# A macaron block on one core: the start, up to the second superblock, rewritten with a held order and a split of the ternary weights into absolute value and sign

## The chip, the cores and the metric

The kernel runs on one core of one Trainium2 chip. The metric is the device time of one execution in microseconds, as a median of runs. The engines are named as in the profile: PE is TensorE (matrix products), PEld its weight loads, DVE is VectorE, ACT is ScalarE, POOL is GpSimd, and SP issues most of the DMAs. Each engine takes its own queue of instructions strictly in order; an instruction that waits holds up all that stand behind it.

## The reference

The input is x of 16 sequences x 256 tokens x 256 features. Three layers follow each other, each with a residual:

```python
x = x + 0.5 * ffn(layernorm(x))
x = x + attention(layernorm(x))      # 16 heads of 16, 4 key groups, causal
x = x + 0.5 * ffn(layernorm(x))      # the same weights again

def ternary_quant(w):
    scale = jnp.mean(jnp.abs(w)) + 1e-8
    return jnp.clip(jnp.round(w / scale), -1.0, 1.0) * scale

def ffn(x):                          # W_up, W_gate: 1024 x 256, W_down: 256 x 1024
    up, gate = x @ ternary_quant(W_up).T, x @ ternary_quant(W_gate).T
    return (silu(up) * gate) @ ternary_quant(W_down).T
```

Before the first product of a weight matrix can run, its mean absolute value must therefore be known over all of its 262,144 elements, and each element must be turned into -1, 0 or 1, by comparing it with plus and minus half the scale.

## The kernel before

The 4096 tokens are cut into eight superblocks of 512. One feed-forward pass over a superblock has eight *units*, f = 0 to 7, each for 128 of the 1024 hidden features, and four *downs*, one for each 128 tokens.

- A unit (`ffn_unit`, line 464) computes `up` and `gate`, four products of 128x512 each (line 451; the normalized input is held as a high and a low f16 half, for two chunks of features). ACT takes the activation of `up` into `th` (line 480), DVE multiplies it with `gate` into `h` (line 481), ACT writes the high f16 half of `h` into `hT` (line 491), and POOL writes the low half (line 492).
- A down (`ffn_down`, line 496) is 16 products of 128x256 with the ternary `td` (line 502), and DVE adds the result to x (line 507). A superblock's four downs are 64 products.

**Order.** A planner (`run`, line 891) writes the steps out in an order, from costs and due times written by hand, with a main chain of units and downs (`ffn_chain`, line 769) and side chains for the norms, the projections and the attention. Behind it a scheduler orders the instructions of each engine again, by its own estimate of their times, unless they are pinned (`pin`, line 223) or of high priority. The result is fixed in the program. Steps for the start are inserted into the main chain at places given by numbers (lines 1047 to 1053).

**The start.** SP issues the loads: x of superblock 0 in one piece, W_up in four, W_gate in one, x of superblock 1, W_down, then the rest (lines 190 to 205). POOL fills constant tiles for the attention. TensorE runs 12 small products to be busy (line 219). The norm of a superblock is: statistics on DVE (line 332), a power of -0.5 on POOL (line 339), the normalization on ACT and DVE (lines 347 and 352), and then, for superblocks 0 and 1, transposes on TensorE and a split into high (ACT) and low (DVE) halves (lines 386 to 389); from superblock 2 on the halves are written into `xparts` (ACT line 364, POOL line 367) and transposed by a DMA.

**The ternary weights before.** `ternary_sums` (line 277) adds up absolute values, on ACT mostly, with a throw-away output. `ternary_scale` (line 298) sums over the partitions by a product with ones (line 301) and makes the two bounds `hi` and `lo`. `ternary_piece` (line 312) makes one quarter of a matrix in two steps:

```python
if engine == "a":
    nc.scalar.activation(dn, wi, AF.Relu, bias=lo, scale=-1.0)
    nc.scalar.activation(dn, dn, AF.Sign)
else:
    by.tensor_scalar(dn, wi, lo, None, ALU.is_lt)      # by: gpsimd or vector
nc.vector.scalar_tensor_tensor(ti, wi, hi, dn, ALU.is_gt, ALU.subtract)
```

So `dn` (is w below -scale/2?) needs the scale. For W_up all four quarters of `dn` are made on DVE; for W_gate one on DVE, two on ACT, one on POOL; for W_down all four on ACT. The second step is always on DVE.

For the projections' weights, DVE finds maxima (`projections_most`, line 980), TensorE transposes them (`mt`, line 998) and later spreads them with a product (`every`, line 1007).

Of the kernel before, what the change touches and what calls it, by code (L numbers as in the profile page):

```python
# [25 lines left out]
ENG_U = "vvvv"  # L26
ENG_G = "vapa"
ENG_D = "aaaa"
NUF = "000000"
NWF = "404000"  # L30
# [8 lines left out]
PINF = 0  # L39
NW4 = 0  # L40
PRE = 0
USUM = 1
GSUM = 0
PING = 0
HPU = 0
GFIRST = 0
PINF1 = 0
TDA = 1
PINK = 1
KM = 2  # L50
KV = 12
PINA = 0
PINM = 1
PINT = 0
NWARM = 12
NWARM2 = 0
NWARM3 = 0
GCUT = 0
# [9 lines left out]
C1 = 1  # L68
C2 = 4
C3 = 5  # L70
TD = 6
DR = 6
DS = 2
PM = 9
# [3 lines left out]
GU = 1  # L78
# [15 lines left out]
NORM = 1024.0  # L94


@with_exitstack
def macaron_kernel(
# [45 lines left out]

    x_t = x.rearrange("(n s) (t p) e -> n p (s t) e", s=2, t=2)
# [44 lines left out]
    load_x(0)  # L190
    for w, w_t in ((wu, w_upT), (wg, w_gateT)):
        for i in range(NCUT if w is wu or GCUT else 1):
            nn = NCUT if w is wu or GCUT else 1
            cut = slice(i * F // nn, (i + 1) * F // nn)
            nc.sync.dma_start(w[:, :, cut], w_t.rearrange("(c p) f -> p c f", p=P)[:, :, cut])
# [13 lines left out]
    nc.vector.tensor_copy(identh, ident)  # L209
    ones = const.tile([P, P], F32, tag="ones", name="ones")  # L210
    nc.vector.memset(ones, 1.0)
    neg_half = const.tile([P, TT], F32, tag="neg_half", name="neg_half")
    nc.vector.memset(neg_half, -0.5)

    def warm(n, name):
        if n:
            pw = bank([P, P], f"warm_{name}")
            for _ in range(n):
                nc.tensor.matmul(pw, ones, ones, start=True, stop=True)

    warm(NWARM, "start")
# [4 lines left out]

    box = {}
# [10 lines left out]
    def constant_rows():  # L238
# [4 lines left out]
        nc.gpsimd.memset(k[KP:KR], 0.0)  # L243
        ku = k[KP:KR].rearrange("p (v u k) -> p v u k", v=3, k=U)
        for which, base in ((EVEN, 0), (ODD, 32)):
            nc.gpsimd.affine_select(
                out=ku[:, which], in_=ku[:, which], pattern=[[0, S // U], [-1, U]],
                compare_op=ALU.is_ge, fill=-MASK, base=base, channel_multiplier=1,
            )
        nc.gpsimd.memset(k[KR : KR + 3], -MROW)  # L250
        nc.gpsimd.memset(v[KP:KR], 0.0)
        vj = v[KP:KR].rearrange("p (j b) -> p j b", b=4)
        nc.gpsimd.affine_select(
            out=vj, in_=vj, pattern=[[1, 32], [0, 4]], compare_op=ALU.not_equal,
            fill=MASK, base=0, channel_multiplier=-1,
        )
        for to in Ks:
            nc.sync.dma_start(
                to[KP : KR + 3].rearrange("p g v k -> p g (v k)"),
                k[KP : KR + 3].unsqueeze(1).to_broadcast([KR + 3 - KP, G, 3 * S]),  # L260
            )
        box["queries"] = v

    def constant_values():
        for v in VT:
            nc.gpsimd.memset(v, 0.0)
            nc.gpsimd.memset(v[:, :, :, D : D + 1], 1.0)
# [9 lines left out]
    def ternary_sums(w, name):  # L277
        if name == "d":
            cuts = [(w[:, : FC // 2], 1), (w[:, FC // 2 :], 1)]
        elif name == "u" or GCUT:  # L280
            fq = F // NCUT
            cuts = [(w[:, :, i * fq : (i + 1) * fq], 0 if i % 2 == 0 and not USUM else 1) for i in range(NCUT - 1)]
            h = fq // 2
            cuts += [(w[:, :, (NCUT - 1) * fq : (NCUT - 1) * fq + h], 0), (w[:, :, (NCUT - 1) * fq + h :], 1)]
        else:
            cuts = [(w[:, : EC // 2], GSUM), (w[:, EC // 2 :], 1)]
        part = small.tile([P, len(cuts)], F32, tag="part", name=f"part_{name}")
        for i, (piece, on_scalar) in enumerate(cuts):
            if on_scalar:
                junk = fp.tile([P] + list(piece.shape[1:]), F16, tag="th", name=f"junk_{name}_{i}")  # L290
                nc.scalar.activation(junk, piece, AF.Abs, accum_out=part[:, i : i + 1])
            else:
                pin(PING and name == "g", nc.vector.tensor_reduce(
                    part[:, i : i + 1], piece, AX.XY, ALU.add, apply_absolute_value=True
                ))
        return part

    def ternary_scale(w, name, part):
        n = w.shape[1] * w.shape[2]
        allsum = bank([P, part.shape[1]], f"allsum_{name}")  # L300
        nc.tensor.matmul(allsum, ones, part, start=True, stop=True)
        tot = small.tile([P, 1], F32, tag="tot", name=f"tot_{name}")
        nc.vector.tensor_reduce(tot, allsum, AX.X, ALU.add)
        s = const.tile([P, 1], F32, tag=f"s_{name}", name=f"s_{name}")
        nc.vector.tensor_scalar(s, tot, 1.0 / (P * n), TERNARY_EPS, ALU.mult, ALU.add)
        hi = small.tile([P, 1], F32, tag="hi", name=f"hi_{name}")
        nc.vector.tensor_scalar(hi, s, 0.5, None, ALU.mult)
        lo = small.tile([P, 1], F32, tag="lo", name=f"lo_{name}")
        nc.vector.tensor_scalar(lo, s, -0.5, None, ALU.mult)
        return s, hi, lo  # L310

    def ternary_piece(wi, ti, hi, lo, name):
        engine = {"u": ENG_U, "g": ENG_G, "d": ENG_D}[name[0]][int(name[1])]
        dn = fp.tile([P] + list(wi.shape[1:]), BF16, tag="tmp", name=f"dn_{name}")
        if engine == "a":
            nc.scalar.activation(dn, wi, AF.Relu, bias=lo, scale=-1.0)
            nc.scalar.activation(dn, dn, AF.Sign)
        else:
            by = nc.gpsimd if engine == "p" else nc.vector
            pin(PINT and engine == "v", by.tensor_scalar(dn, wi, lo, None, ALU.is_lt))  # L320
        nc.vector.scalar_tensor_tensor(ti, wi, hi, dn, ALU.is_gt, ALU.subtract)


    def norm_stages(n, name, factor, finish, early=False):
# [4 lines left out]
        def stats():  # L329
            st = small.tile([P, TT, nc.vector.BN_STATS_DIM], F32, tag="st", name=f"st_{name}")  # L330
            for t in range(TT):
                pin(PINA if name[0] == "a" else PINF1 if name in ("f0_1", "f0_2") else PINF if name[:2] == "f0" else 0, nc.vector.bn_stats(st[:, t, :], xs[n][:, t, :]))
            for t in range(TT):
                nc.vector.bn_aggr(mv[:, t, :], st[:, t, :])
            ve = small.tile([P, TT], F32, tag="ve", name=f"ve_{name}")
            nc.vector.tensor_scalar(
                ve, mv[:, :, 1], LN_EPS, 1.0 / (factor * factor), ALU.add, ALU.mult
            )
            nc.gpsimd.tensor_tensor(rstd, ve, neg_half, ALU.pow)

        def normalize():
            on_scalar = 2 if name in ("first", "second") else NACT0 if early else NACT
            shift = small.tile([P, TT], F32, tag="shift", name=f"shift_{name}")
            nc.vector.scalar_tensor_tensor(shift, mv[:, :, 0], -1.0, rstd, ALU.mult, ALU.mult)
            for t in range(TT):
                if t < on_scalar:
                    nc.scalar.activation(
# [3 lines left out]
                else:  # L351
                    nc.vector.tensor_scalar(  # L352
# [6 lines left out]
    def ffn_norm(n, name, tag="xT", early=False):  # L359
# [3 lines left out]
        def high(xn):  # L363
            nc.scalar.copy(parts[:, 0].rearrange("p c t e -> p t c e"), xn.rearrange("p t (c e) -> p t c e", c=EC))  # L364

        def low(xn):
            nc.gpsimd.tensor_tensor(  # L367
# [9 lines left out]
    def early_norm(n, name):  # L377

        xT = lnp.tile([P, 2 * EC * TT, P], F16, tag="xT", name=f"xT_{name}")
        view = xT.rearrange("p (a c t) q -> p a c (t q)", a=2, c=EC)  # L380

        def transposed(xn):
            for c in range(EC):
                pt = bank([P, TT, P], f"xt_{name}_{c}")
                for t in range(TT):
                    nc.tensor.transpose(pt[:, t, :], xn[:, t, c * P : (c + 1) * P], ident)
                p2 = pt.rearrange("p t q -> p (t q)")
                nc.scalar.copy(view[:, 0, c, :], p2)
                nc.vector.tensor_tensor(view[:, 1, c, :], p2, view[:, 0, c, :], ALU.subtract)

        return view, norm_stages(n, name, NORM, [transposed])
# [43 lines left out]
    def ffn_prepare(key):  # L435
        n, p = key
        if key == order[1]:
            view, stages = early_norm(n, "second")
        else:
            view, stages = ffn_norm(n, f"f{p}_{n}", early=p == 0 and n < EARLY_F)  # L440
# [5 lines left out]
    half_done = {}  # L446

    def products(key, f, w, acc):
        for c in range(EC):
            for a in range(2):  # L450
                nc.tensor.matmul(  # L451
# [4 lines left out]
    def ffn_up(key, f):  # L456
        name = f"{key[1]}_{key[0]}_{f}"
        if key == order[0] and f < 6:
            warm(int(NUF[f]), f"u{f}")
        up = bank([P, 512], f"u_{name}")  # L460
        products(key, f, tu, up)
        half_done[key, f] = up

    def ffn_unit(key, f):
        n, p = key
        name = f"{p}_{n}_{f}"
        if f == 0:
            hidden[key] = hp.tile([P, FC, 2, 512], F16, tag="hT", name=f"hT_{p}_{n}")
        hT = hidden[key]
        if (key, f) not in half_done:  # L470
            ffn_up(key, f)
        up = half_done.pop((key, f))
        gate = bank([P, 512], f"g_{name}")
        if key == order[0] and f < 6:
            warm(int(NWF[f]), f"g{f}")
        products(key, f, tg, gate)
        th = fp.tile([P, 512], F32, tag="th", name=f"th_{name}")
        h = fp.tile([P, 512], F32, tag="h", name=f"h_{name}")
        if key in order[:SILU]:
            nc.scalar.activation(th, up, AF.Silu, scale=scales["one_u"])  # L480
            nc.vector.scalar_tensor_tensor(h, gate, scales["per_u"], th, ALU.mult, ALU.mult)
# [620 lines left out]
```

## Time and profile before

| what | value |
|---|---|
| median of 3 runs | 566.72 us (565.25 to 567.57) |
| the profiled execution's own time | 563.64 us |
| its span in the profile | 561.9 us |
| mean granted TensorE clock | 0.988 |
| PE busy | 539.4 us, 96% of the span |
| DVE, ACT, POOL busy | 433.2, 376.5, 355.0 us (77%, 67%, 63%) |
| first product of superblock 0 (`u`, unit 0) | begins at 13.28 us |
| first products of superblock 1 | begin at 33.23 us |
| first down product of superblock 0 | begins at 47.43 us |
| last down product of superblock 0 ends, unit 5 of superblock 1 begins | 54.59 us in the chain |

How to read it: a row of the profile page's groups gives line, engine, operation, `out<-in` by the program's tile names, the shapes, the count, then the busy time, the mean of one in ns, and the idle time of the engine before it with what ended it. A row of the timeline has the start in us, the duration, the engine, the line, the operation and how many were merged. A row of a table by windows has, for each stretch, the busy time of each engine, the granted TensorE clock (1.00 is full), the busy share of the DMA engines and their GB/s. In the names of tiles, `Qs` is also where the raw W_up, W_gate and W_down lie during the start.

### The profile page before, as it was taken

How to read it: one execution, taken by the hardware profiler on the slowest of the kernel's cores; microseconds unless marked ns; L12 is line 12 of the kernel's file. 1: busy time of each engine (PE TensorE's matmuls, PEld its weight loads, DVE VectorE, ACT ScalarE, POOL GpSimd, SP SyncE). 2: the span in 40 equal slices, each digit the busy share in tenths (PEclk: the TensorE clock that was granted, in tenths of full speed). 3: DMA queues.
4: the chain of work that ended last, by engine and by line, in shares of the span. 5: the costliest groups of instructions: out<-in, count | busy, mean ns of one | idle time of the engine just before them, and what ended most of it. 6: DMA issues, size and time to landing. Idle time of an engine off the chain costs nothing.

```text
span 561.9 us, 12132 instructions
## 1 busy us (share of the span) xinstructions
PE 539.4 (96%) x4593; PEld 331.1 (59%) x4593; DVE 433.2 (77%) x1027; ACT 376.5 (67%) x658; POOL 355.0 (63%) x380
## 2 busy tenths in 40 slices
PE   6979999989999999999999999899999999999997
PEld 5436556647555665655665664566645666565565
DVE  6988878977989899878877798459965697846663
ACT  5894747487689668677856749765599445875642
POOL 4466869556489658766845539854489534865542
PEclk8899999999999999999999999999999999999999
DMA  8933268571059059047339003572023840020201
GB/s 297 297 43 56 38 156 154 125 167 44 3 160 144 1 147 159 3 126 142 47 96 190 12 3 38 135 170 38 3 40 66 205 87 22 12 65 14 67 28 48
DMA packets 119316, 51.25 MB, mean 91 GB/s; under 512 B 85173, under 2 KB 119001, under 8 KB 119257
## 3 DMA queue, kind: packets, MB, share of 16 engines
q1 hardware_dynamic: 118825, 50.08, 40.4%
q8 instruction: 36, 0.59, 0.4%
q10 hardware_dynamic: 432, 0.39, 0.3%
q14 instruction: 23, 0.19, 0.1%
HBM read 22.41 MB, written 14.68 MB: 66 GB/s over the span
## 4 chain that ended last, share of the span: by engine, by line
PE 72%; ACT 10%; DVE 9%; DMA 5%; POOL 2%; issue 2%; SPq 0%; DVEq 0%; ACTq 0%; POOLq 0%
PE d L502 18%; PE u L451 15%; PE g L451 14%; PE o L706 6%; PE s L611 6%; PE st L675 5%; PE qkv L525 4%; ACT pT L676 2%; DMA Qs<-prows 2%; PE ot L722 2%; DVE xn_f L352 1%; DVE h L486 1%; DVE tmp L485 1%; ACT hT L491 1%; DVE tops L625 1%
## 5 line engine op out<-in xcount | busy, mean ns | idle before, releaser
L492 POOL TENSOR_TENSOR hT<-h,hT 128x512 f16<-128x512 f32 x128 | 149.2, 1171 | 88.8 <-ACT hT L491 88.0
L676 ACT ACTIVATE pT<-st,exp_scale 128x512 f32<-128x512 f32 x192 | 119.8, 698 | 26.1 <-PE st L675 26.0
L502 PE MATMUL d<-td,hT 128*128 128x256 f16 x1024 | 122.4, 273 | 0.2 <-ACT pT L676 0.2
L625 DVE TENSOR_REDUCE tops<-s 128x8 f32<-128x512 f32 x160 | 103.1, 678 | 16.1 <-PE s L611 15.7
L451 PE MATMUL u<-xT_f,tu 128*128 128x512 f16 x448 | 115.2, 379 | 0.3 <-DVE h L486 0.3
L451 PE MATMUL g<-xT_f,tg 128*128 128x512 f16 x448 | 115.3, 379 | 0.0
L684 POOL TENSOR_SCALAR_AFFINE_SELECT pT<-pT 128x512 f32<-128x512 f32 x128 | 80.5, 637 | 54.7 <-ACT pT L676 51.7
L491 ACT CAST hT<-h 128x512 f16<-128x512 f32 x128 | 79.5, 621 | 49.2 <-DVE h L486 39.0
L502 PEld LDWEIGHTS <-hT 128*128 128x128 f16 x1024 | 98.4, 98 | 18.0 <-issue 0.5
L485 DVE SCALAR_TENSOR_TENSOR tmp<-th,u 128x512 f32<-128x512 f32 x96 | 65.5, 684 | 50.3 <-ACT th L483 49.8
L483 ACT ACTIVATE th<-u,half_u 128x512 f32<-128x512 f32 x96 | 66.2, 692 | 42.8 <-PE u L451 42.4
L451 PEld LDWEIGHTS <-tg 128*128 128x128 f16 x512 | 50.2, 98 | 61.8 <-issue 1.7
L451 PEld LDWEIGHTS <-tu 128*128 128x128 f16 x512 | 47.6, 99 | 43.7 <-issue 2.9
L486 DVE SCALAR_TENSOR_TENSOR h<-g,tmp 128x512 f32<-128x512 f32 x96 | 65.7, 685 | 5.7 <-PE v L573 0.5
L675 PE MATMUL st<-Qs,ks 99*128 99x512 f16 x192 | 54.1, 380 | 5.4 <-DMA Qs<-prows 2.8
L611 PEld LDWEIGHTS <-Qs 96*128 96x128 f16 x896 | 50.9, 116 | 12.7 <-issue 3.0
L611 PE MATMUL s<-ks,Qs 96*128 96x64 f16 (+2 forms) x896 | 53.3, 208 | 0.0
L706 PE MATMUL o<-pT,vt 128*32 128x128 f32 (+1 forms) x1024 | 49.4, 329 | 0.0
L706 PEld LDWEIGHTS o<-pT,vt 128*32 128x32 f32 x1024 | 28.5, 109 | 25.1 <-issue 8.6
L507 DVE SCALAR_TENSOR_TENSOR x<-d,so,x 128x256 f32<-128x256 f32 x64 | 30.4, 478 | 16.5 <-PE d L502 16.0
L525 PE MATMUL qkv<-xT_a,wparts 128*128 128x512 f16 x144 | 34.7, 379 | 2.0 <-DMA xT_a<-xparts_a 1.9
L367 POOL TENSOR_TENSOR xparts_f<-xn_f,xparts_f 128x1024 f16<-128x1024 f32 x14 | 29.9, 2132 | 9.4 <-ACT xparts_f L364 9.2
(163 smaller groups left out, 605.1 us busy)
## 6 DMA issues: line engine op xcount, KB each, us to landing
qd<-sp SPq DMA_DIRECT2D x32, 256.0 KB, 2.6
Qs<-qd SPq DMA_DIRECT2D x64, 128.0 KB, 3.5
ks<-kd SPq DMA_DIRECT2D x48, 128.0 KB, 4.1
x<-in_x SPq DMA_DIRECT2D x8, 512.0 KB, 8.7
out<-x SPq DMA_DIRECT2D x32, 128.0 KB, 3.0
kd<-sp SPq DMA_DIRECT2D x16, 128.0 KB, 2.5
Qs<-in_w_upT SPq DMA_DIRECT2D x4, 256.0 KB, 4.9
Qs<-in_w_gateT SPq DMA_DIRECT2D x1, 1024.0 KB
```

What stands on the lines that cost most here:

```text
L451: nc.tensor.matmul(acc, w[:, c, f * P : (f + 1) * P], ffn_ready[key][:, a, c, :], start=(c == 0 and a == 0), stop=(c == EC - 1 and a == 1),)
L485: nc.vector.scalar_tensor_tensor(tmp, th, 1.0, up, ALU.add, ALU.mult)
L486: nc.vector.scalar_tensor_tensor(h, gate, 0.25 / (NORM * NORM), tmp, ALU.mult, ALU.mult)
L491: nc.scalar.copy(hT[:, f, 0, :], h)
L492: nc.gpsimd.tensor_tensor(hT[:, f, 1, :], h, hT[:, f, 0, :], ALU.subtract)
L502: nc.tensor.matmul(acc, hT[:, f, a, t * P : (t + 1) * P], td[:, f, :], start=(f == 0 and a == 0), stop=(f == FC - 1 and a == 1),)
L611: nc.tensor.matmul(sc[:, at : at + n, :], Qs[0:KR, b // 4, g * P : (g + 1) * P, b % 4], k[:, g, which, first * U : (first + n) * U], start ...
L625: nc.vector.tensor_reduce(peaks[q][:, u, :], sc, AX.X, ALU.max)
L675: nc.tensor.matmul(sc, keys, mov, start=True, stop=True)
L676: nc.scalar.activation(pT[:, u, :].rearrange("p (h b j) -> p h b j", h=4, b=4), sc.rearrange("p (h j b) -> p h b j", h=4, b=4), AF.Exp, sc ...
L684: nc.gpsimd.affine_select(out=v, in_=v, pattern=[[0, 4], [1, P]], compare_op=ALU.is_ge, fill=0.0, base=0, channel_multiplier=-1,)
L706: pin(not first, nc.tensor.matmul(at[:, half * P :], v[:, 2 * s + half, g, :], moving, start=half == 0, stop=half == 1, tile_position=(0, ...
```

## The change

The start is written anew up to and with the norm statistics of superblock 2, and all that is issued in this stretch keeps the written order on every engine: a wrapper around the engines pins each instruction while a flag is set. What comes behind it is ordered by planner and scheduler as before.

- **Loads.** x of superblock 0 comes in two halves, W_gate in four pieces instead of one; the statistics of superblock 0 run by halves, with two powers on POOL instead of one.
- **Ternary weights.** w becomes `(|w| > scale/2) * (half of the sign of w)`. The half signs (+0.5 or -0.5) need no scale. They are made by POOL from the raw weights, one `tensor_scalar` of two operations for each quarter (128x512), but for the first eighth of W_up, which DVE makes. The absolute values are kept: ACT's sums write them into a tile (`sizes`, in the space of a later `hT`); for W_down they overwrite the raw weights. DVE then needs one instruction for a quarter, with two inputs in SBUF, as before. The `dn` instructions on ACT and DVE are gone. A factor of two that the half signs bring is moved into the scales.
- **Sums.** Some are on DVE (two quarters of W_gate, an eighth of W_up). The sum over partitions accumulates piece by piece in one PSUM bank. The scale and bounds are each made by one DVE instruction from that bank.
- **Activation table.** A one-element Silu is the first activation, so that its table is loaded at the start; the two table loads of the first stretch (at 0.78 and at 16.93 us before, 1.28 us each) become one.
- **Products.** The `up` products of units 0 and 1 are interleaved, chunk by chunk. From there the order is written out: `up` products run one or two units ahead of `gate`, with the sign, size and ternary pieces between them. Seventeen warming products instead of 12 at the start and three before the first `gate`; the eight between units are gone.
- **Constants.** All constant tiles of the attention are filled on POOL before the first norm.
- **W_down.** Its signs, sums and ternary pieces are inserted as steps of the planner after superblock 0 (places 0, 1, and 2 to 5 of the main chain); the projections' maxima and the products behind them come later.

In the built program, POOL's queue after the norm of superblock 0 is: sign of W_up (eighth 2), of W_gate (quarter 1), W_up (2), W_gate (2); then low half of unit 0, sign W_up (3), low 1, sign W_gate (3), low 2, sign W_up (4), the power for superblock 1, low 3, sign W_gate (4), lows 4 to 7; the power for superblock 2, the low half of unit 0 of superblock 1, four signs of W_down, `xparts` of superblock 2, and the lows of units 1 to 7. On ACT the normalization and `xparts` of superblock 2 stand just ahead of the first sum of W_down, which stands ahead of the activation of unit 1 of superblock 1. On PE the product that adds the first half of W_down's sum (`all_d`) stands between units 0 and 1 of superblock 1, the second inside the last products of unit 4; the 64 down products of superblock 0 follow; `mt` and `every` come after them. From the downs of superblock 1 on, PE's order is that of the kernel before.

The core of the diff:

```diff
+    class Engine:
+        def __getattr__(self, name):
...
+            def issue(*args, **kwargs):
+                ins = fn(*args, **kwargs)
+                if box["in_order"]:
+                    tc.keep_in_program_order(ins)
+                return ins
...
-    load_x(0)
+    for s in range(2):
+        nc.sync.dma_start(xs[0][:, 2 * s : 2 * s + 2], x_t[0][:, 2 * s : 2 * s + 2])
...
+    def half_sign(engine, to, w):
+        engine.tensor_scalar(to, w, 0.0, 0.5, ALU.is_ge, ALU.subtract)
+
+    def ternary(t, size, cut, sign):
+        vector.scalar_tensor_tensor(t, size, cut, sign, ALU.is_gt, ALU.mult)
+
+    def affine(name, acc, factor, eps):
+        to = const.tile([P, 1], F32, tag=name, name=name)
+        vector.tensor_scalar(to, acc, factor / (E * F), eps, ALU.mult, ALU.add)
+        return to
...
+    def sum_by_scalar(size, w, part, i, lo, hi):
+        scalar.activation(cut_w(size, lo, hi), cut_w(w, lo, hi), AF.Abs, accum_out=part[:, i : i + 1])
...
+    g_ternary(0, 1)
+    g_ternary(1, 2)
+    s_g = affine("s_g", all_g, 1.0, TERNARY_EPS)
+    warm(NWARM2, "second")
+    units[0].gate()
+    units[1].gate()
+    u_ternary(2, 4)
...
+    units[0].join()
+    size_by_scalar(size_g, wg, 4, 6)
+    split(0)
+    u_sign(gpsimd, 4, 6)
+    next_up(2)
+    g_ternary(2, 4)
+    next_up(3)
...
+    split(3)
+    g_sign(gpsimd, 6, 8)
+    units[4].gate()
+    u_ternary(6, 8)
...
+    g_ternary(6, 8)
+    units[5].join()
...
+    third = ffn_prepare(order[2])
+    third[0]()
+    vector.tensor_copy(identh, ident)
+    box["in_order"] = False
+    for stage in third[1:]:
+        stage()
...
     def ternary_down_sums():
+        for i in range(4):
+            rows = slice(2 * i, 2 * i + 2)
+            half_sign(gpsimd, sign[:, rows], wd[:, rows])
+        for i in range(2):
+            rows = slice(4 * i, 4 * i + 4)
+            scalar.activation(wd[:, rows], wd[:, rows], AF.Abs, accum_out=part[:, i : i + 1])
+
+    def ternary_down_scale():
+        all_d = bank([P, 1], "all_d")
+        for i in range(2):
+            total(all_d, box["part_d"][:, i : i + 1], i == 0, i == 1)
```

## The prediction

> **What bounds the kernel now.** I read the page's head, then the start by windows, then the chain and the waits of the first 56 us.
>
> ```profile
> PE 539.4 (96%) x4593; PEld 331.1 (59%) x4593; DVE 433.2 (77%) x1027; ACT 376.5 (67%) x658; POOL 355.0 (63%) x380
> ...
> PE   6979999989999999999999999899999999999997
> ```
>
> From the fourth slice on PE is full nearly everywhere. Only the start and the end have room, and a microsecond by which PE's queue comes later at 54 us is a microsecond of the end.
>
> ```profile
> 5.00:10.00 5.00, 1.57 (x10) 1.29 (x9) 3.03 (x15) 3.19 (x10) 2.17 (x4) 0.90 1.04 381
> 10.00:15.00 5.00, 4.18 (x18) 3.52 (x19) 5.00 (x16) 2.76 (x6) 0.00 (x0) 0.50 1.09 352
> 15.00:20.00 5.00, 4.33 (x14) 1.62 (x14) 5.00 (x22) 3.78 (x6) 2.07 (x2) 0.57 1.10 347
> ...
> 35.00:40.00 5.00, 1.84 (x9) 0.64 (x7) 4.06 (x7) 5.00 (x9) 2.58 (x2) 0.97 0.00 0
> 40.00:45.00 5.00, 4.61 (x16) 1.93 (x17) 4.19 (x9) 3.84 (x8) 5.00 (x5) 0.68 0.59 108
> ```
>
> Columns: PE, PEld, DVE, ACT, POOL busy, then the granted clock. Before 20 us PE waits and runs at half clock; DVE is full. POOL is nearly idle there: that is the room the change uses. A second hole, 35 to 40, is followed by half clock again (0.68 is a mean of 0.50 and 1.00): after some 3 us idle the next products take twice their 216 ns.
>
> ```profile
> 39.14 0.98 DVE most L984 x3
> ...
> 40.39 0.37 PE mt L998
> 40.76 1.71 PE u L451 x4
> ...
> 47.50 7.09 PE d L502 x64
> 54.59 0.86 PE u L451 x4
> ```
>
> ```profile
> PE mt L998 <- DVE most L991: 3.5, 1, 3.5
> ```
>
> The hole is one small product: `mt`, ahead of unit 2 in PE's queue, waits for a late DVE result. The downs end at 54.59; from there PE's order is unchanged, so I compare this point.
>
> **The new start, part by part.** I lay out the changed queues with the rows' durations: 0.69 us for `th`, 0.74 for `h` and for a ternary quarter, 0.62 for the high half, 0.864 for four full-clock products, 1.03 for a power, and POOL's:
>
> ```profile
> L492 POOL TENSOR_TENSOR hT<-h,hT 128x512 f16<-128x512 f32 x128 | 149.2, 1171 | 88.8 <-ACT hT L491 88.0
> L684 POOL TENSOR_SCALAR_AFFINE_SELECT pT<-pT 128x512 f32<-128x512 f32 x128 | 80.5, 637 | 54.7 <-ACT pT L676 51.7
> ```
>
> ```profile
> 18.94 1.73 POOL L320 TENSOR_SCALAR dn_g<-Qs,lo_g 128x512 bf16<-128x512 f32 x1 [2.01 <-DVE tu L321]
> ```
>
> The old queues laid out so reach the first down at 47.7; the trace has 47.4.
>
> *To the first gate product: 2.7 us earlier.* POOL's constants end near 6.8, then two powers, so the first norm is done at 9.9 instead of 10.6. `cut_u` comes at 9.8; two eighths of `tu` are ready at 10.8 (was 11.6). The first input's last low half is done at 12.1 (was 15.2), because statistics and sums no longer stand ahead of it on DVE. The sums of W_gate (two on ACT to 12.75, two on DVE at 0.70 to 13.3), `cut_g` and two eighths of `tg` end at 14.8: the first gate product stands at 14.8 instead of 17.5. The pieces of W_gate help here; the table load that goes (1.28 us) is off the path by then. Halves of x cost SP 0.5 us more issue, hidden by the data rate (345 GB/s).
>
> *Units 0 to 7: the lead is lost on POOL.* **The unknown price** is a half sign on POOL: two operations on 128x512, for seven quarters and an eighth of W_up and W_gate, and four quarters of W_down. Nearest from below is the select of the same size (0.64 us), from above two passes of the one-operation `tensor_scalar` (3.46). I take that row itself, 1.73: same operation, size and engine; it was one quarter, now it is eleven. The trace shows nothing nearer. Low 0 starts at 17.3. To the last gate sign POOL does four lows (4.7), four signs (6.9), one power (1.0) and waits 1.2 for `h` of unit 2: 31.1. What DVE and ACT do behind it in order (ternary 0.74, `h` 0.74, high 0.62, `th` 0.69, two high halves, `h`, low half of superblock 1's input) ends at 36.6. Superblock 1's whole input was ready at 34.2 before: **2.4 us late**, where PE alone could have been done with superblock 0 near 27.9.
>
> *The new wait: 9.4 us.* Unit 0 of superblock 1 ends at 37.6. Next in PE's queue stands the first half of W_down's sum, and all other units and downs stand behind it. Its chain: DVE has the statistics of superblock 2 ahead of `h` of unit 0 (to 39.4), then the variance (39.9); POOL's power (41.0), the low half (42.1), two signs of W_down (3.46, to 45.6); ACT's normalization and `xparts` (1.1 + 1.04) lie beside those; then ACT's sum with its read, 1.05 + 0.19: 46.9. The sign must precede the sum, which overwrites the raw weights. Before, this hole was 3.5 us.
>
> *Units 1 to 4 and the downs.* Eight groups at 0.864, part of them at half clock after the hole: 47.4 to 55.1. The second sum is long done; `cut_d` and a ternary quarter (0.15 + 0.74, and latencies) hold the downs until 56.4. 64 products at 0.107 end at 63.2, against 54.6: **+8.7**. `mt` and `every` now come after the downs instead of before: +0.5.
>
> *What the change removes.* ACT loses 5.4 us of W_down's `dn` and 2.7 of W_gate's, DVE some 2.4; ACT was full from 20 to 42. Their cover is POOL's queue, which is later than both, so they are worth nothing here.
>
> *POOL beside DVE.* The low halves at 26.64 took 5.25 for four (4.7 by the mean), beside two ternary pieces; I add 0.3, since most of this falls where POOL waits anyway. Sum: 8.7 + 0.5 + 0.3 = **9.5**, or 573.1 on the profiled execution's own 563.64. That lies 3.1 under the median; on 566.72 it gives **576.2**.
>
> *Two rules of the Trainium skill.* "GPSIMD Engine Reference", section 4.1 (Engine selection), calls one-input operations on GpSimd roughly line-rate; the row says 1.73 us for 512 elements, far from it, and by the rule the sum would be near that of the 0.64 row, about +5. "SBUF — State Buffer", section "Who interferes with whom", speaks against the change: a DVE instruction with two SBUF inputs and a GpSimd one that reads SBUF exclude each other, the later one waiting for the whole other. The trace agrees in part (four low halves 5.25 us; tiny DVE operations of 1.13 and 1.04 us at 24.43 and 29.75); by the rule each of five ternary pieces beside POOL's chain could add 0.74, so about +13.
>
> **Rivals.**
> 1. *Fast signs* (0.64 to 0.9 us). For: POOL's select. Against: the one `tensor_scalar` row. The lead lasts longer (unit 0 of superblock 1 ends at 33.7), but the wait for W_down's sum stays at 7.8 us, since statistics, power, normalization, `xparts` and sum stand in series without the signs. Downs end at 59.0: +4.4 + 0.5, **571.6**.
> 2. *Slow signs* (2.2 to 3.5 us). For: two operations instead of one. Each 0.1 us is paid about 1.1 to 1.8 times over: +14.7 at 2.5 (**581.4**), +23 at 3.46 (589.7).
> 3. *Not slower: PE alone paces superblock 0.* If DVE, ACT and POOL all keep up, PE has 14 groups (12.1) and eight transposes (1.0) from 14.8: 27.9; unit 0 of superblock 1 ends near 30.0. The sum's chain without POOL's backlog is 5.8; then 0.5 + 7.7 + 1.3 + 6.8: 52.1, and 0.5 for `mt` and `every`: 2.0 us gained, **564.7**; a clock that stays full through the hole gives 1.7 more. It decides from the point where that unit ends before 32.0. For: ACT and DVE lose 10 us of work. Against: POOL alone has 13.8 us between 17.3 and 31.1.
> 4. *The order is held, yet not where it matters*: the flag is off behind superblock 2's statistics, and `all_d` is put by the scheduler. This is within the forecast.
>
> **Chances.** Forecast (signs 0.9 to 2.2; 574 to 579): 0.62. Rival 1: 0.12. Rival 2: 0.18. Rival 3: 0.08, of which 0.03 faster by over 0.5% (2.8 us, about what a measurement of this kernel can tell from no change) and 0.05 within. Range: 568.5 (rival 1 on the own time's base) to 587 (signs near 3).
>
> **What will show it.** POOL's rows for `signs` give the price, 1.73 expected. The first gate product should stand near 14.8; POOL should be full from 17 to 50; PE should wait 8 to 10 us for `all_d`, the largest wait of the start, with a clock near 0.5 after it; the downs should end near 63. If PE's hole at `all_d` is under 4 us, the layout of the queues is wrong; if it is there and the time does not grow, some later slack has absorbed it.

## The result, and the profile after

The changed kernel takes **580.08 us** (median of 4 runs, 578.54 to 581.09), beside 565.99 for the kernel before on the same chip (565.16 to 567.57). The ratio is 1.0243, with a 95% interval of 1.0208 to 1.0278: 14.1 us slower, where 9.5 were forecast. The profiled execution took 578.54 us, with a span of 576.4 (before: 563.64 and 561.9).

The head of the page of the changed kernel, with the busy times and PE's row of 40 slices:

```profile
PE 542.6 (94%) x4609; PEld 331.9 (58%) x4609; DVE 434.5 (75%) x1023; ACT 369.9 (64%) x649; POOL 375.4 (65%) x392
...
PE   8665899998999999999999999899999999999997
```

A slice is 14.4 us. From the sixth on PE is as full as before, so nearly all that is lost lies in the first 72 us: the second to fourth slices were 9, 7 and 9 and are 6, 6 and 5, while the first rose from 6 to 8. POOL got 20 us more work, ACT lost 7, and DVE's sum is about the same.

The start by windows (PE, PEld, DVE, ACT, POOL busy, then the granted clock, the DMA share and GB/s):

```profile
10.00:15.00 5.00, 4.34 (x28) 2.85 (x27) 4.41 (x15) 3.38 (x8) 5.00 (x3) 1.00 1.09 353
15.00:20.00 5.00, 4.91 (x24) 2.25 (x24) 3.34 (x8) 3.15 (x6) 2.79 (x3) 1.00 1.10 349
...
25.00:30.00 5.00, 1.39 (x5) 0.44 (x6) 2.41 (x4) 1.89 (x4) 4.23 (x4) 0.74 0.57 168
30.00:35.00 5.00, 5.00 (x17) 2.15 (x16) 4.12 (x6) 2.28 (x4) 3.96 (x3) 0.57 0.53 75
...
40.00:45.00 5.00, 0.00 (x0) 0.00 (x0) 3.95 (x13) 1.89 (x5) 4.25 (x5) 0.95 0.00 2
45.00:50.00 5.00, 0.76 (x3) 0.56 (x4) 0.26 (x1) 2.60 (x4) 5.00 (x4) 0.50 0.01 2
50.00:55.00 5.00, 5.00 (x14) 1.79 (x13) 0.75 (x1) 2.39 (x5) 4.02 (x3) 0.53 0.00 0
```

The first 20 us are better than before: the clock is full (it was 0.50 and 0.57) and the first gate product stands at 15.1 us instead of 17.5. From 40 to 49 PE does nothing at all, with POOL busy nearly throughout (4.25 and 5.00 of 5 us), and from 50 to 55 it works at half clock. The clock is half within superblock 0 as well, from 27.4 to 34.3 us, after PE's waits for ternary pieces. That stretch does not set the end of superblock 0: in the two runs with products of no use, whose code is the same up to there, the clock was half from 23.9 to 34.2, and in two stretches of 3.4 us each, and unit 0 of superblock 1 ends at 39.6 and 39.7, against 39.5 here. The wait list of the start names the pause, and the chain shows what led to it:

```profile
PE all_d L140 <- ACT Qs L140: 9.7, 1, 9.7
```

```profile
42.06 0.20 POOL rstd_f L140
42.26 0.80 issue
43.06 1.15 POOL hT L140
44.21 3.80 POOL signs_d L140 x2
48.01 0.02 issue
48.03 1.16 ACT Qs L140 x2
49.19 0.04 issue
49.24 0.59 PE all_d L140 x2
...
59.20 1.63 DVE td L140
60.83 0.04 issue
60.87 7.15 PE d L140 x64
68.02 0.11 PE mt L140
```

(In the changed kernel nearly every instruction has line 140, that of the wrapper; read the tiles.) The power of superblock 2, a low half, two signs of W_down and ACT's sum follow each other while the products of units 1 to 4, whose inputs are ready, stand behind `all_d`. The downs end at 68.0, where they ended at 54.6: 13.4 us. The same down products stay 14.0 late in superblock 1, up to 16.9 in between, and 14.7 at the end.

### The profile page after: what moved, and what is told of

It reads as the page before. It is cut to its first block, busy times and chain, and to the rows that moved or that the text cites. A ratio compares the mean times of both kernels' runs of the same rounds, so it can differ in the third digit from the quotient of the medians.

```text
span 576.4 us, 12168 instructions
## 1 busy us (share of the span) xinstructions
PE 542.6 (94%) x4609; PEld 331.9 (58%) x4609; DVE 434.5 (75%) x1023; ACT 369.9 (64%) x649; POOL 375.4 (65%) x392
## 4 chain that ended last, share of the span: by engine, by line
PE 69%; DVE 12%; ACT 8%; POOL 5%; DMA 3%; issue 2%; SPq 0%; DVEq 0%; ACTq 0%; POOLq 0%
PE d L140 17%; PE u L140 14%; PE g L140 13%; PE o L140 6%; PE s L140 6%; PE st L140 5%; PE qkv L140 3%; ACT pT L140 3%; DVE h L140 3%; PE ot L140 2%; DMA Qs<-prows 2%; POOL hT L140 1%; DVE xn_f L140 1%; DVE st_f L140 1%; DVE tmp L140 1%
## 5 line engine op out<-in xcount | busy, mean ns | idle before, releaser
L140 POOL TENSOR_SCALAR_AFFINE_SELECT pT<-pT 128x512 f32<-128x512 f32 x128 | 80.6, 637 | 54.7 <-ACT pT L140 54.2
L140 DVE TENSOR_REDUCE tops<-s 128x8 f32<-128x512 f32 x160 | 103.0, 677 | 15.6 <-PE s L140 15.2
L140 PE MATMUL o<-pT,vt 128*32 128x128 f32 (+1 forms) x1024 | 49.4, 329 | 0.0
L140 DVE SCALAR_TENSOR_TENSOR x<-d,out_scale,x 128x256 f32<-128x256 f32 x64 | 30.4, 477 | 15.7 <-PE d L140 15.2
```

Source lines behind the costliest of these rows:

```text
L140: ins = fn(*args, **kwargs)
```

## The experiments

The theory of the prediction: POOL, with the new signs, is late; PE's queue is in order, so that it stands for W_down's sum; the pause costs clock too. Its rivals: the wait is only a place where a general lateness shows, or DVE and ACT are as late as POOL. Times against the changed kernel are differences of the two ratios to the kernel before, times 566 us; since each ratio is known to some 0.2 to 0.5%, a difference under about 3 us is not clear of noise by the times alone, and the place where the last down product of superblock 0 ends in the profile (68.0 in the changed kernel) is given as a second measure. That place is from one execution, and what the half clock took from it differs between executions by about 1 us (last section).

**The sum, the cut and the pieces of W_down behind unit 3.** The three numbers are places in the planner's main chain.

```diff
-TD = 2
-TDS = 1
-DS = 1
+TD = 5
+TDS = 4
+DS = 0
```

> W_down's sum product, its cut and its four ternary pieces stand behind unit 3 of superblock 1 in program order instead of behind unit 0; nothing else changes. Theory (PE stands still because its queue is in order and the sum comes late): units 1 to 3 run in the hole, PE's wait for all_d falls from 9.7 us to 4 or 5, the downs end near 64 instead of 68.0, and the time falls by 4 us, to about 576. Rival (the wait is only where a general lateness of DVE, ACT and POOL shows): the wait goes elsewhere, the downs end near 68, and the time stays within 1 us of 580.

Measured: 577.16 us, ratio 1.0185 (1.0141 to 1.0229), 3.3 us less; the downs end at 65.4, 2.6 us earlier. PE's wait:

```profile
PE all_d L140 <- ACT Qs L140: 5.9, 1, 5.9
```

The units do run in the hole, so the wait is PE's order and not a general lateness. The gain is smaller than expected since the four ternary pieces of W_down now ran beside POOL's low halves and held the downs three times (1.63, 0.78 and 0.20 us).

**Four signs from POOL to DVE.**

```diff
-    u_sign(gpsimd, 4, 6)
+    u_sign(vector, 4, 6)
...
-    g_sign(gpsimd, 6, 8)
+    g_sign(vector, 6, 8)
```

> The four half signs of the last two quarters of W_up and W_gate are done by DVE instead of POOL, at the same places of the order. Theory (POOL's queue, with signs of 1.92 us, paces superblock 0 and holds the sum of W_down): POOL loses 7.8 us in superblock 0, DVE gets about 2; unit 0 of superblock 1 ends 4 to 5 us earlier than 39.5, all_d follows, and the time falls by 5 to 7 us, to about 574. Rival (DVE and ACT are as late as POOL): unit 0 ends less than 2 us earlier and the time falls by less than 2.

Measured: 572.92 us, ratio 1.0110 (1.0072 to 1.0148), 7.5 us less; the downs end at 63.0. PE's timeline:

```profile
35.16 0.38 PE L140 MATMUL g<-xT_second,tg 128*128 128x512 f16 x1
45.24 0.59 PE L140 MATMUL all_d<-part_d,ones 128*128 128x1 f32 x2 [9.70 <-ACT Qs L140]
```

The last product of unit 0 of superblock 1 ends at 35.5 instead of 39.5, and the wait for `all_d` is 9.70 us again: the chain to W_down's sum simply moved with POOL. Of the 5.0 us at the downs' end 4.0 are this; the other 1.0 is the clock, which was half for 3.5 us after the pause here and for 5.5 in the changed kernel. POOL paces superblock 0; DVE does such a sign in 0.41 us where nothing holds it up (two of the four, the others took 0.72 and 0.97), POOL in 1.92.

**Products of no use in the pause.**

```diff
         unit.join()
+        if key == order[1] and f == 0:
+            pw = bank([P, P], "warm_wait")
+            for _ in range(18):
+                tensor.matmul(pw, ones, unit.th[:, :P], start=True, stop=True)
```

> 18 products of no use, on the curve of unit 0 of superblock 1, stand ahead of W_down's sum in PE's queue, in the time in which PE waits anyway. Theory (the pause itself brings the half clock after it): the granted clock stays near 1.00 from 45 to 55, units 1 to 4 take 7 us instead of 9, the downs end near 65 and the time falls by 2.5 to 3 us, to about 577. Rival (the clock falls for another reason, or the units wait for DVE anyway): the clock is still near 0.5 there, or the time stays within 0.7 us of 580.

Measured: 579.01 us, ratio 1.0218 (1.0182 to 1.0255), the downs end at 68.0: no gain that can be told. The products took only 4.3 us; 4.8 us of pause were left, and the clock fell to half at 47.8. The run did not test the theory, since there was still a pause; so twice as many:

```diff
-            for _ in range(18):
+            for _ in range(36):
```

> As the run with 18 products of no use in PE's wait, but with 36 of them: those 18 took only 4.3 us and left 4.8 us of pause, and the clock fell all the same. 36 should run from 40.2 to 48.8. Theory (the pause brings the half clock): PE's wait for all_d is under 1 us, the granted clock stays near 1.00 from 45 to 60, units 1 to 4 take 7 us instead of 9, the downs end near 65.5 instead of 68.0, and the time falls by 2 to 3 us. Rival (the units' pace after the pause comes from DVE, ACT or POOL, or the clock falls for another reason): the downs end near 68 again and the time is that of the run with 18 products, about 579.

Measured: 577.06 us, ratio 1.0198 (1.0162 to 1.0233), 2.5 us less; the downs end at 65.7. The table by windows, columns as above:

```profile
45.00:50.00 5.00, 4.20 (x37) 3.83 (x36) 0.41 (x2) 2.75 (x5) 5.00 (x3) 1.00 0.02 5
50.00:55.00 5.00, 5.00 (x25) 2.25 (x23) 1.50 (x2) 3.56 (x6) 5.00 (x4) 1.00 0.00 0
```

With the pause filled (0.8 us left), the clock stays full and units 1 to 4 take 7.2 us from first to last product (49.63 to 56.84) instead of 9.7 (49.69 to 59.36), after a sum at the same time (49.4). The half clock is a consequence of the pause and costs 2.3 us at the downs' end.

**Ternary pieces with one large input.** The prediction gave 0.3 us to POOL and DVE holding each other up. The timeline of DVE in the changed kernel (start, duration, and the idle time before) speaks for more:

```profile
20.84 1.63 DVE L140 SCALAR_TENSOR_TENSOR tu<-sizes,cut_u,signs_u 128x512 f16<-128x512 f32 x1 [2.49 <-POOL signs_u L140]
24.84 0.74 DVE L140 SCALAR_TENSOR_TENSOR tg<-sizes,cut_g,signs_g 128x512 f16<-128x512 f32 x1
28.84 0.75 DVE L140 SCALAR_TENSOR_TENSOR tu<-sizes,cut_u,signs_u 128x512 f16<-128x512 f32 x1 [2.59 <-POOL signs_u L140]
32.87 1.64 DVE L140 SCALAR_TENSOR_TENSOR tg<-sizes,cut_g,signs_g 128x512 f16<-128x512 f32 x1 [0.88 <-POOL signs_g L140]
```

and that of POOL has, at the two long ones, a low half that was ready when the sign ended:

```profile
20.78 1.15 POOL L140 TENSOR_TENSOR hT<-h,hT 128x512 f16<-128x512 f32 x1
...
32.80 1.16 POOL L140 TENSOR_TENSOR hT<-h,hT 128x512 f16<-128x512 f32 x1
```

The long pieces end 0.54 and 0.55 us after those low halves do (22.47 against 21.93, 34.51 against 33.96): most of a piece's 0.74 us comes only behind the low half. The first try to test this:

```diff
-        vector.scalar_tensor_tensor(t, size, cut, sign, ALU.is_gt, ALU.mult)
+        vector.tensor_scalar(t, size, cut, sign[:, 0, 0:2].bitcast(F32), ALU.is_gt, ALU.mult)
```

> The ternary pieces read only the absolute values from SBUF, and one sign value of the piece as a scalar, so that they wait for the same POOL instruction but have one large SBUF input instead of two; this leaves the signs out of the ternary values. Theory (a DVE instruction with two SBUF inputs and a POOL instruction exclude each other): the pieces that took 1.63 and 1.64 us take about 0.55, unit 0 of superblock 1 ends about 2 us earlier than 39.5, and the time falls by 2 to 3 us, to about 577.5. Rival (those pieces were long only because they wait for the sign itself): pieces behind POOL's next instruction still take over 1 us, and the time falls by 0.5 us at most.

Measured: 576.64 us, ratio 1.0197 (1.0143 to 1.0250), 2.6 us less; the downs end at 65.7. The time came as expected, but not for the reason given: an undisturbed piece takes 0.54 us, and the two beside POOL's low half still take 1.36 and 1.37, so 0.82 us of hold-up remains. The theory in its narrow form, two large inputs in SBUF, fell. The gain is that of shorter pieces: unit 0 of superblock 1 ends 0.5 us earlier, where 2 were expected, and the downs wait 0.2 us for `td` instead of 1.5.

**POOL held instead.**

```diff
-    split(1)
+    units[1].high()
+    u_ternary(4, 6)
+    held = small.tile([P, 2], F16, tag="held", name="held", bufs=1)
+    gpsimd.tensor_copy(held[:, 0:1], tu[:, 0, 4 * P : 4 * P + 1])
+    units[1].low()
```

and the same at the piece behind the last sign of W_gate.

> In two places POOL is made to wait until DVE's ternary piece is done, by a copy of one element of that piece ahead of its next low half: at the piece behind the sign at 20.84 and at the one behind the sign at 32.87. The work is otherwise the same. Theory (a ternary piece that is ready together with a POOL instruction stands until that one has ended): both pieces take 0.75 us instead of 1.63; PE's waits for tu and tg there become about 0.9 shorter, POOL is 0.9 to 1.1 us later each time, and the time stays within 2 us of 580 on either side. Rival (the two pieces are long for a reason of their own): they still take 1.6 us.

Measured: 579.42 us, ratio 1.0231 (1.0201 to 1.0260); the downs end at 68.5. DVE's timeline:

```profile
22.19 0.75 DVE L140 SCALAR_TENSOR_TENSOR tu<-sizes,cut_u,signs_u 128x512 f16<-128x512 f32 x1 [2.50 <-POOL signs_u L140]
26.23 1.71 DVE L140 SCALAR_TENSOR_TENSOR tg<-sizes,cut_g,signs_g 128x512 f16<-128x512 f32 x1 [0.82 <-POOL signs_g L140]
...
33.77 0.75 DVE L140 SCALAR_TENSOR_TENSOR tg<-sizes,cut_g,signs_g 128x512 f16<-128x512 f32 x1 [0.89 <-POOL signs_g L140]
```

Both pieces, at 22.19 and 33.77, take 0.75 once no POOL instruction starts with them. The piece at 26.23, 0.74 in the changed kernel, now takes 1.71: a low half stands beside it. The hold-up is of whole POOL instructions, as expected, and goes where the two engines meet.

**Signs of one operation.**

```diff
-        engine.tensor_scalar(to, w, 0.0, 0.5, ALU.is_ge, ALU.subtract)
+        engine.tensor_scalar(to, w, 0.0, None, ALU.is_ge)
```

> The changed kernel with POOL's signs made by one operation (is_ge) instead of two (is_ge, subtract): all of POOL's instructions stay where they are, the sign values are 1 and 0 instead of 1/2 and -1/2, so the negative ternary values are left out. Theory (the forecast missed part of the time because a sign of two operations takes 1.92 us, not the 1.73 of the one-operation row): the signs take about 1.73, unit 0 of superblock 1 ends 0.6 to 0.9 us earlier than 39.5, W_down's sum 1 to 1.4 earlier than 49.24, and the time falls by 1 to 2 us, to about 578.5; the rest of the miss stays. Rival (the second operation costs POOL nothing, the earlier row was only of another output type): the signs stay at 1.92 and the time at 580.

Measured: 575.29 us, ratio 1.0153 (1.0131 to 1.0174), 5.1 us less; the downs end at 65.1. POOL's groups of the first 70 us (count, busy time, mean ns), first the changed kernel, then this one:

```profile
L140 POOL TENSOR_SCALAR signs_g<-Qs 128x512 f16<-128x512 f32 x4 | 8.3, 2065 | 0.5 <-DMA Qs<-in_w_gateT 0.5
L140 POOL TENSOR_SCALAR signs_d<-Qs 128x512 f16<-128x512 f32 x4 | 7.6, 1922 | 0.0
L140 POOL TENSOR_SCALAR signs_u<-Qs 128x512 f16<-128x512 f32 x3 | 5.8, 1918 | 0.0
```

```profile
L140 POOL TENSOR_SCALAR signs_g<-Qs 128x512 f16<-128x512 f32 x4 | 6.6, 1639 | 1.2 <-DMA Qs<-in_w_gateT 1.2
L140 POOL TENSOR_SCALAR signs_d<-Qs 128x512 f16<-128x512 f32 x4 | 5.9, 1497 | 0.0
L140 POOL TENSOR_SCALAR signs_u<-Qs 128x512 f16<-128x512 f32 x3 | 4.5, 1485 | 0.0
```

The second operation costs 0.43 us, and the one-operation sign 1.49, less than the row of 1.73 that the prediction took (its output was bf16, and DVE worked beside it; which of the two made the difference was not tried). The time fell by more than expected. Part of that is the clock: in this execution it returned to full at 51.9, in the changed kernel's at 54.7, though the sum came only 0.7 us earlier. Another part is W_down's first piece, which was held less: it takes 1.10 us instead of 1.63, and the downs wait 0.34 us for it instead of 1.50. Against that, this execution had half clock from 10.9 to 14.3 and a first gate product 1.4 us later, which the shorter signs made good by the end of unit 0 (39.6, against 39.5). The downs end 2.9 us earlier; how much of the 5.1 us is the signs alone is therefore open.

**W_down early, on ACT.** On top of the four signs on DVE:

```diff
+    scalar.activation(td[:, 0:2], wd[:, 0:2], AF.Sign)
+    scalar.activation(td[:, 2:4], wd[:, 2:4], AF.Sign)
...
+    scalar.activation(wd[:, 0:4], wd[:, 0:4], AF.Abs, accum_out=part_d[:, 0:1])
...
-        s_d = affine("s_d", all_d, 1.0, TERNARY_EPS)
+        s_d = affine("s_d", all_d, 0.5, 0.5 * TERNARY_EPS)
```

> On top of the run with four signs on DVE: W_down's signs and sums are done by ACT (sign, 0.63 us a quarter, written into td) inside superblock 0 instead of by POOL and ACT behind the norm of superblock 2. Theory (PE's in-order wait for W_down's sum is the largest part of the loss): the wait for all_d goes, PE runs on from unit 0 of superblock 1 at full clock, the downs end near 50 to 52 instead of 63.0 there and 54.6 before the change, and the time is 562 to 565, under that of the kernel before. Rival (unit 0's successors wait for something else, such as ACT or the norm of superblock 2): PE pauses elsewhere and the time stays above 567.

Measured: **564.11 us**, ratio 0.9959 (0.9942 to 0.9976): under the kernel before. PE's timeline:

```profile
34.63 0.28 PE L140 MATMUL all_d<-part_d,ones 128*128 128x1 f32 x2
...
45.26 1.92 PE L140 MATMUL d<-td,hT 128*128 128x256 f16 x16 [2.00 <-DVE td L140]
48.90 5.40 PE L140 MATMUL d<-td,hT 128*128 128x256 f16 x48 [1.72 <-DVE td L140]
```

No wait for `all_d` is left, the clock is full from 14.3 us on, and the downs end at 54.3, over 2 us later than expected, with two waits for ternary pieces of W_down (2.0 and 1.7 us) beside POOL's low halves. Between this kernel and the one with four signs on DVE alone lie 1.5%, some 8.5 us, and 8.7 at the downs' end, where the four signs brought 5.0: the largest single part of the loss is that the sum of W_down came behind POOL's queue and the norm of superblock 2, with the half clock that the pause brought.

**All late signs off POOL.** The signs of W_down on DVE, the late ones of W_up and W_gate on ACT:

```diff
-    u_sign(gpsimd, 4, 6)
+    scalar.activation(cut_w(sign_u, 4, 6), cut_w(wu, 4, 6), AF.Sign)
...
+    half_sign(vector, td[:, 0:2], wd[:, 0:2])
```

> All eight late signs off POOL: the last two quarters of W_up and W_gate by ACT (sign, with scales of their own for units 4 to 7), W_down's by DVE in superblock 0, its sums by ACT. POOL keeps the low halves, the powers and the first signs. Theory (POOL's queue): superblock 0 ends 1 to 2 us earlier than with the signs on DVE, no wait for all_d, the downs end near 50 and the time is 561 to 564. Rival (DVE or ACT become the bound of superblock 0): the same time as the run with W_down on ACT, or up to 3 us more.

Measured: 564.00 us, ratio 0.9976 (0.9954 to 0.9998), the downs end at 54.7: the rival's first half, the same as with W_down on ACT. Superblock 0 did not end earlier (unit 0 of superblock 1 ends at 35.9, with the signs on DVE at 35.5). Once POOL is relieved of its late signs, who takes them matters little.

**Cut and pieces of W_down sooner; the norm of superblock 2 behind.**

```diff
-TDS = 1
-DS = 1
+TDS = 2
+DS = 0
...
-    for stage in third[1:]:
-        stage()
...
+        if i == 3:
+            for stage in third[1:]:
+                stage()
```

> On top of the run with four signs on DVE and W_down on ACT: the first of W_down's sums one unit later on ACT, the product, cut and ternary pieces of W_down behind unit 1 of superblock 1 in one go, and the normalization of superblock 2 behind them in program order. There the downs waited twice for ternary pieces of W_down (2.0 and 1.7 us) that stood beside POOL's low halves and took 5.7 us for four. Theory (those pieces are late because they start late and run beside POOL): they start near 41 instead of 43.5, the two waits shrink by 2 us in all, the downs end near 52 instead of 54.1, and the time is about 562. Rival (later slack absorbs it): 564 as there.

Measured: 564.42 us, ratio 0.9972 (0.9953 to 0.9991). The downs end at 52.0, 2.3 us earlier, and the span is 1.3 shorter (561.2), yet the medians do not tell the two kernels apart. The 2.3 us are not those that were expected. 0.9 of them are there at the first gate product (15.2 instead of 16.2): in this execution the clock was full at the start, in the other it was half from 10.9 to 14.3. Another 1.0 is there when superblock 1 begins, since ACT's first sum of W_down no longer stands ahead of superblock 1's input (PE waited 1.34 us for it, now 0.30). The two waits for `td` are still 1.68 and 1.72, 0.3 less in all: the pieces started earlier and were held nearly as long.

**Both, and the whole norm of superblock 2 behind.** The edits of the run above, the late signs of W_up and W_gate on ACT as two runs above, and:

```diff
-    third[0]()
...
-            for stage in third[1:]:
+            for stage in third:
```

> As the run with cut and pieces of W_down sooner, and the late signs of W_up and W_gate on ACT (with scales of their own for units 4 to 7) instead of DVE; the whole norm of superblock 2 stands behind the pieces in program order and outside the held order. Theory: with DVE free of all late signs and POOL of the long low half beside the pieces, the downs end 1 to 2 us earlier than there, near 51, and the time is about 561. Rival (DVE was not the bound of superblock 0, or the norm of superblock 2 now comes late): 562 to 565.

Measured: **562.39 us**, ratio 0.9936 (0.9912 to 0.9960): the fastest, against 1.0243 for the changed kernel. The downs end at 49.5. Its head, and its windows at the place of the earlier hole and pause:

```profile
PE 537.6 (96%) x4609; PEld 330.5 (59%) x4609; DVE 435.0 (78%) x1025; ACT 373.3 (67%) x657; POOL 361.2 (65%) x384
```

```profile
35.00:40.00 5.00, 5.00 (x28) 2.60 (x26) 2.10 (x6) 5.00 (x9) 3.63 (x4) 1.00 0.13 26
40.00:45.00 5.00, 3.71 (x30) 2.57 (x28) 5.00 (x6) 1.81 (x4) 3.51 (x3) 1.00 0.43 81
```

The clock is full, and where the kernel before had a hole of 3.5 us and the changed kernel a pause of 9.7, PE stands for two ternary pieces of W_down, 0.54 and 0.75 us. Of the 5.1 us that its downs are earlier than before the change, 3.6 are left at the end; PE waits 1.7 us for a result of ACT (`full`, ahead of product `v`) behind superblock 1's second down, where the kernel before has no wait. It differs from the run above in two things, signs on ACT and the place of the norm; which of them did it was not separated.

**One part alone, on the kernel before.**

```diff
-GCUT = 0
+GCUT = 1
```

> The kernel before, with one part of the change alone: W_gate is loaded and summed in more pieces. Theory (in the kernel before the hole ahead of unit 2 of superblock 1 and ACT's and DVE's queues set the end, the loads do not): the first gate product moves by less than 1 us, PE's wait for mt stays, and the time is within 1.5 us of the kernel before. Rival (the pieces are where the earlier start comes from): the first gate product stands 1 to 2 us earlier and the time falls by 1 to 2 us.

Measured: 565.15 us, ratio 0.9986 (0.9967 to 1.0005): no difference that can be told. The first gate product stands at 18.7 (1.2 later, not within the 1 us expected), PE's wait for `mt` is 3.0 instead of 3.5. The pieces of W_gate alone neither bring the early start nor cost the 14 us.

## Why the prediction was right, and what it missed

The direction and the mechanism held. The size was 14.1 us instead of 9.5; on the profiled executions' own times it is 14.9. 580.08 lies within the range of 568.5 to 587, but 1.1 us above the 574 to 579 that the forecast gave for signs of 0.9 to 2.2 us. By its steps:

- *To the first gate product.* Forecast 14.8, measured 15.1, 2.4 us earlier than before. Right.
- *The lead is lost on POOL.* Right, and shown by the four signs on DVE. **Mis-sized:** the last gate sign ends at 32.8 instead of 31.1. The price of a half sign, 1.73, was from a row of one operation; two take 1.92, and one of them 2.36 beside a DVE piece. Four signs make 8.1 us where 6.9 were counted. Unit 0 of superblock 1 ends at 39.5 instead of 37.6. POOL was not full from 17 to 50 as forecast: from 35 to 40 it was busy for 2.16 of 5 us, since behind its last sign the chain runs over DVE, ACT and PE, as laid out.
- *POOL beside DVE, 0.3 us.* **The step that failed most.** Two pieces on the chain were held 0.9 us each, the first piece of W_down 0.9 once more (the downs waited 1.5), and one sign 0.4. By the Trainium skill, "SBUF — State Buffer", section "Who interferes with whom", the later one of the two engines waits for the whole other; the rows agree (1.63 and 1.64 against 0.74), and the run that held POOL agrees. By that rule the prediction counted five pieces, 3.7 us, and a time of about +13. Three pieces on the chain were held, 2.7 us, each beside a POOL instruction that started with it; the time came near +13 all the same, with the dearer signs, the longer half clock and the wait for `full` below. Not all of this adds to the miss: from the last gate sign to the end of unit 0 the layout allowed 6.5 us, and 6.7 were taken with one of the hold-ups inside.
- *The new wait, 9.4 us.* Measured 9.7, for the product named, with the chain named. Right; with W_down early it goes, and 8.5 us with it.
- *Units 1 to 4.* **Mis-sized:** 9.0 us up to the second product of the sum, instead of 7.7. The half clock was expected for part of them; it lasted until 54.7, 5.5 us after work began again. Filling the pause gave back 2.3 us.
- *Cut and ternary piece.* The downs start at 60.9 instead of 56.4; 0.8 of that is new here, the held piece, whose 0.9 is counted above. The sum of all: 13.4 at the downs' end against 8.7 (and 0.3).
- *After the downs, 0.5.* Right for `mt` and `every`: the first down of superblock 1 is 14.0 late. Then PE waits 1.3 us for ACT's `full` at 91.0, ahead of product `v`, where the kernel before has no wait; the forecast had no such term. 14.7 are left at the end of the kernel, and 0.4 us more lie outside the span. Why ACT is late there was not followed further.
- *What the change removes is worth nothing.* Right for the changed kernel: ACT waits 15 us for `h` in the first 75 us.

Of the rivals, "slow signs" gave 581.4 at 2.5 us, nearly the time measured; but the signs cost 1.92, within the forecast's bounds, and the rest came from the hold-ups and the clock. A right time from that rival would have been right for a wrong reason. "Not slower" fell for this kernel; the best version, with POOL's backlog gone and W_down's chain early, is 0.6% faster than the kernel before.

## What to carry to other kernels

An operation moved to an idle engine is not free if that engine's queue also carries what the next stage waits for: lay out the whole queue of the receiving engine, with its other work, up to the first thing that another engine needs in order. Put a product that depends on a long chain as late in PE's queue as its result allows, or start its chain early; here W_down's chain alone was worth 1.5%. Where DVE and POOL work side by side on SBUF, count whole instructions of the other engine for every piece that becomes ready together with one.

## What was not expected of the hardware

- The granted clock changes in steps of one length: it was half for 10.2 us after the changed kernel's pause (44.5 to 54.7), for 6.8 with 18 products in it (47.8 to 54.7), for 3.4 in the kernel before (39.7 to 43.2) and for 13.6 in the run that held POOL (41.9 to 55.5); these are three, two, one and four times 3.41. The Trainium skill, "TensorE: Matmul & The Clock Gate", section "What's actually happening", gives a free-running window of 3413 ns, and these runs agree. So nearly equal pauses cost different amounts, by where they fall: behind a pause of 9.7 us PE worked at half clock for 5.5 us in the changed kernel and for 3.5 with four signs on DVE (half from 38.5 to 48.7), and behind one of 9.6 for 6.1 us in the run that held POOL.
- The start shows the same: five of the profiled executions (four signs on DVE, POOL held, signs of one operation, W_down early on ACT, all late signs off POOL) had half clock from about 11 to 14.5 us, with the first gate product at 16.2 to 16.5, and the changed kernel and its other versions did not (15.0 to 15.5). In the first, second and fourth of the five the code up to there is that of the changed kernel.
- A DVE `tensor_scalar` with one large input is held by POOL just as the piece with two: 1.36 us against 0.54. It took 0.41 for 256 elements and 0.54 for 512, so 256 more cost 0.13, where the two-input piece (0.48 and 0.74) pays 0.26. The Trainium skill, "VectorE: DVE Perf Modes", section "Mode 2×_2P — use both read ports for one tensor", describes a mode for such an instruction that takes both read ports; the two rates fit it, and no run here shows the ports themselves.
- POOL's `tensor_scalar` on 512 elements takes 1.49 us with one operation and 1.92 with two; DVE's with two takes 0.41 to 0.42 when nothing holds it.
